# Shared convolution products seeded in a second PSUM bank, with the gate chain moved ahead

## The chip, the cores and the metric

The kernel runs on one core of a Trainium2 chip. The metric is the device time of one execution in microseconds. Engines: PE is TensorE (PEld its weight loads), DVE is VectorE, ACT is ScalarE, POOL is GpSimd, SP is the engine that issues most of the DMAs. Line numbers are those of the kernel before.

## The reference

An adaptive-LayerNorm block on x of shape (4, 1024, 2048), in float32. Six modulation vectors come from `c` (4 x 2048) and `wmod` (2048 x 6*2048):

```python
mod = (_silu(L0_c) @ L0_wmod).reshape(L0_c.shape[0], 6, 1, -1)
sa, ca, ga, sb, cb, gb = (mod[:, 0], ..., mod[:, 5])
ga = (2 * (ga >= 0) - 1) * jnp.maximum(jnp.abs(ga), 0.25)   # gb likewise
h = _layernorm(x, axis=-1) * (1 + ca) + sa
x = x + ga * _L0_attn_ref(h, ...)
h = _layernorm(x, axis=-1) * (1 + cb) + sb
x = x + gb * _L0_ffn_ref(h, ...)
```

`_L0_attn_ref` is a state-space layer: from 64 complex parameters it makes a kernel K of 2048 taps (four response sums over the states at 2048 frequencies, then an inverse FFT), convolves every row of h causally with K along the last axis, and adds `D * h`. `_L0_ffn_ref` is a linear layer of 2048 x 2048 with bias, with 16 low-rank updates of rank 16 added, each weighted by `coeffs * scales`.

## The kernel before

The 4096 rows of x are taken as 32 tiles of 128 rows, called rows here (r = 0 to 31). The kernel has two stages: in the first, every row goes through normalization, convolution, gate and residual, and is written to a scratch tensor `x1d`; in the second, 16 units of two rows go through the linear layer (`ffn_unit`, L750), written as seven products of half-size blocks.

**The convolution as matrix products.** The taps are laid out as a Toeplitz matrix of 128 x 128 blocks; even and odd blocks of the output are made from three families of products instead of four. `toeplitz` (L233) builds them: `s4` computes the response sums (`s4rp`, L175) and the taps, these go to DRAM (`kd`), come back as a shifted matrix `kb` (L258), are reversed by PE (`kbps`, L263), and become three pairs of f16 tensors, high and low part, `kh` and `kl` (L284, L285), one pair for each family f = 0, 1, 2.

**A row.** `stats` (L540) and `normalize` (`n`, L557) run on DVE. `conv_prep` (L566 on) transposes n on PE in four chunks of four blocks (`tp`, L578), ACT evacuates each with scale and shift (`t`, L582), DVE adds neighbouring blocks (`sm`, L590), and ACT and DVE split t and sm into f16 high and low parts `hc` and `hs` (L592, L593). `conv_mm` then runs 108 products in six groups (two halves q of the output, three families): family 0 from hs gives a sum that odd and even blocks share. It lies in PSUM tile `ya`, ACT copies it to SBUF (`qs`, L627), PE adds family 1 to it in place, and makes family 2 in `yb` alone; DVE adds `qs` to `yb` (L631). The odd blocks are then multiplied by the gate (L633), the even ones straight from `ya` (L640), and x is added with a running sum (L641). `conv_post` writes y to `x1d` and takes the second variance (L660).

**PSUM.** Three pools share the eight banks for the whole kernel: `acc` with five banks (all products), `tps` with two (transposes and small products), `mps` with one (`modps`).

**Before the gate is known.** `wmod` is 48 MB for its first three sections, read by 48 loads into two pools of three buffers each (`wm`, `wms`) and multiplied in L317 (`modps`). Section 1 (scale) comes first, then the shift, then the gate. Rows 0 and 1 (`EARLY = 2`) are convolved meanwhile without shift and gate, their products alternating with modps products (`pace`, `ROWC`). `shift_conv` makes the convolution of the shift (`gsp`, L397) and `shift_add` (L414) adds it to both rows. When section 2 is summed, `mod_gate` computes the gate on DVE and ACT (L342 to L347), `gate_tile` spreads it over the partitions by products with rows of the identity (`gps`, L674, `gat`, L675), and `conv_late` (L650, L651) finishes rows 0 and 1. Row 2's convolution runs at the same place; the constant `GCOL` says how many of its columns may stand ahead of gps in PE's order.

**The order of the work.** A scheduler orders each engine's instructions from the program text; `tc.issue_after(ins)` keeps what is traced inside it behind `ins` on that engine, as an order and not as a wait. Inside `conv_mm`, `tick` is called ten times a row, and each call does what `PLAN` says for it: N a part of the next row's `conv_prep`, P the `conv_post` of the row before, T statistics, F the first part of the row after next, S one step of the fill. The fill is the work for the second stage: the low-rank weights are prepared (`prep_lora`), merged into the linear weights in eight parts (`merge`, `lps`, L486, `we`, L488, `wch`, L514), and the other three sections of wmod are multiplied.

Of the kernel before, what the change touches and what calls it, by code (L numbers as in the profile page):

```python
# [24 lines left out]
P = 128  # L25
D = 2048
# [8 lines left out]
class Net:  # L35
    def __init__(self, ctx, tc, io):
        self.ctx, self.tc, self.nc, self.io = ctx, tc, tc.nc, io
        self.cst = ctx.enter_context(tc.tile_pool(name="cst", bufs=1))
        self.dram = ctx.enter_context(tc.tile_pool(name="scr", bufs=1, space=DRAM))
        self.acc = ctx.enter_context(tc.tile_pool(name="acc", bufs=ACC, space=PSUM))  # L40
        self.tps = ctx.enter_context(tc.tile_pool(name="tps", bufs=TPS, space=PSUM))
        self.mps = ctx.enter_context(tc.tile_pool(name="mps", bufs=1, space=PSUM))
# [33 lines left out]
    def s4(self, pool):  # L76
# [69 lines left out]
        rp = self.tps.tile([P, 16, 8], F32, tag="t", name="s4rp")  # L146
        w = 512
        yield
        cps = [[self.acc.tile([P, w], F32, tag="a", name="s4cs") for _ in range(2)] for _ in range(2)]
# [16 lines left out]
        for n, (cc, sc) in enumerate(cps):  # L166
# [4 lines left out]
            yield  # L171
            for c in range(w // P):
                out = rp.rearrange("p (h g) v -> p g h v", h=2)[:, 4 * n + c]
                for i, x in enumerate((wr[n], wi[n])):
                    nc.tensor.matmul(  # L175
                        out, x[:, ds(P * c, P)], cf[:, i],
                        start=(n, c, i) == (0, 0, 0), stop=(n, c, i) == (1, 3, 1), skip_group_check=True,
                    )
        r = T([P, 8, 16], "s4R")
        v.tensor_copy(r.rearrange("p v k -> p k v"), rp)  # L180
# [52 lines left out]
    def toeplitz(self, pool):  # L233
# [23 lines left out]
        src = bass.AP(tensor=kd.tensor, offset=kd.offset + 1, ap=[[1, P], [1, D]])  # L257
        nc.gpsimd.dma_start(out=kb, in_=src)  # L258
        self.kb = kb
        yield  # L260
        for q in range(4):
            ps = self.acc.tile([P, 512], F32, tag="a", name="kbps")
            nc.tensor.matmul(ps, rev, kb[:, ds(512 * q, 512)], start=True, stop=True)  # L263
            (v.tensor_copy if q % 2 else nc.scalar.copy)(kb[:, ds(512 * q, 512)], ps)
# [4 lines left out]
        self.kf = {}  # L269
        for f in (0, 2, 1):  # L270
            hi = self.kpool.tile([P, HC * P], F16, tag=f"kh{f}", name=f"kh{f}")
            lo = self.kpool.tile([P, HC * P], F16, tag=f"kl{f}", name=f"kl{f}")
            h3, l3 = (x.rearrange("p (m t) -> p m t", t=P) for x in (hi, lo))
            if f == 0:
                src = ev
            else:
                src = pool.tile([P, 2, 512], F32, tag="kdif", name="kdif")
                src = src.rearrange("p a (c t) -> p (a c) t", t=P)
                if f == 1:
                    v.tensor_scalar(src[:, 0:1], ev[:, 0:1], -1.0, None, MUL)  # L280
                    v.tensor_tensor(src[:, 1:], od[:, 0 : HC - 1], ev[:, 1:], SUB)
                else:
                    v.tensor_tensor(src, od, ev, SUB)
            v.tensor_copy(h3, src)  # L284
            v.tensor_tensor(l3, src, h3, SUB)  # L285
            self.kf[f] = hi, lo
        yield
# [36 lines left out]
    def mod_column(self, pool, home, name, plus_one):  # L324
# [3 lines left out]
        nc.scalar.copy(row, self.modps)  # L328
# [9 lines left out]
    def mod_gate(self, pool, name, bias=None):  # L338
# [8 lines left out]
        v.scalar_tensor_tensor(g, g, 1.0, m, SUB, MUL)  # L347
# [62 lines left out]
    def shift_add(self, pool, ys):  # L410
        g = pool.tile([P, D], F32, tag="gat", name="gsb")
# [55 lines left out]
    def merge(self, pool, tmp, c):  # L467
# [11 lines left out]
        for h in range(2):  # L479
            for q in range(4):  # L480
                ps = self.acc.tile([P, 512], F32, tag="a", name="lps")
# [54 lines left out]
    def stats(self, pl, x, tag):  # L536
# [8 lines left out]
        if tag in ACTNORM:  # L545
            mb = pl["sm"].tile([P, 1], F32, tag="mb" + tag, name="mb" + tag)
            v.scalar_tensor_tensor(mb, mv[:, 0:1], -1.0, rs, MUL, MUL)
            return mb, rs
        return mv, rs

    def normalize(self, pl, x, st, tag):
        n = pl["n"].tile([P, D], F32, tag="n", name="n" + tag)
        m, rs = st
        if tag in ACTNORM:
            self.nc.scalar.activation(n, x, AF.Identity, bias=m, scale=rs)
        else:
            self.nc.vector.tensor_scalar(n, x, m[:, 0:1], rs, SUB, MUL)  # L557
        return n
# [6 lines left out]
    def conv_prep(self, pl, r, x, st, out, shift=True):  # L565
# [8 lines left out]
        for c0 in range(0, NC, 4):  # L574
# [16 lines left out]
            for (hi, lo), src, sl in ((hc, t, slice(c0, c0 + 4)), (hs, sm, slice(c0 // 2, c0 // 2 + 2))):  # L591
                nc.scalar.copy(hi[:, sl], src)  # L592
# [3 lines left out]
    def conv_mm(self, pl, hs, x, tick, early, pace):  # L596
        nc, v = self.nc, self.nc.vector
        hc, hs = hs
        y = pl["y"].tile([P, D], F32, tag="y", name="y")
# [5 lines left out]
        def family(ps, f, q, first):  # L605
            pf = ps.rearrange("p j t -> p (j t)")
            last = 4 * q + 3
            for i in range(last + 1):
                o = P * max(0, i - 4 * q)
                k0 = P * max(0, 4 * q - i)  # L610
                with pace(3 * (512 - o)):
                    for x, z in ((0, 0), (0, 1), (1, 0)):
# [3 lines left out]
                            start=first, stop=(i == last and (x, z) == (1, 0)), skip_group_check=True,  # L616
                        )
                        first = False
# [3 lines left out]
        for q in range(2):  # L622
            jj = slice(4 * q, 4 * q + 4)
            pa = self.acc.tile([P, 4, P], F32, tag="a", name="ya")
            family(pa, 0, q, True)
            qs = pl["t"].tile([P, 4, P], F32, tag="qs", name="qs")
            self.lasta = nc.scalar.copy(qs, pa)  # L627
            tick()
            pb = self.acc.tile([P, 4, P], F32, tag="a", name="yb")
            family(pb, 2, q, True)  # L630
            self.lastv = v.tensor_tensor(yv[:, jj, 1, :], pb, qs, ADD)  # L631
            if not early:
# [534 lines left out]
```

## Time and profile before

| | |
|---|---|
| median of 3 runs | 2139.6 us (2136.27 to 2143.98) |
| profiled execution, its own time | 2141.87 us |
| its span | 2140.1 us |
| PE busy | 2082.4 us (97%) |
| DVE busy | 1308.4 us (61%) |
| ACT busy | 923.7 us (43%) |
| mean granted clock of PE | 0.988 |
| DMA | 484.11 MB, 226 GB/s |

The profile is one execution. The first stage takes the span's first 919 us (the first product of the second stage starts there), the second stage the rest. Digits in the profile's slices are tenths of a slice of 53.5 us. A group's row gives its busy time, the mean of one instruction in ns, and the engine's idle time before it with what ended it; in a timeline the last bracket is that idle time.

### The profile page before, as it was taken

The page shows a single profiled execution, that of the slowest core. Times are in us where ns is not written, and L with a number is a line of the kernel's source. Part 1 is how long each engine was busy: PE and PEld are TensorE (multiplying, and loading weights), DVE is VectorE, ACT ScalarE, POOL GpSimd, SP SyncE. Part 2 cuts the span into 40 slices and gives each one's busy share as a digit, 9 for nine tenths or more (in the row PEclk, how much of TensorE's full clock was granted, in tenths as well). Part 3 has the DMA queues.
Part 4 walks back from the last instruction along what each step waited for, and adds up shares of the span by engine and source line. Part 5 has one row for each costly group of instructions (what it writes and reads, how often), then busy time and mean ns, then how long its engine had stood idle before and what let it go on. Part 6 is the DMA issues. An engine that isn't in the chain of part 4 may idle for free.

```text
span 2140.1 us, 28438 instructions
## 1 busy us (share of the span) xinstructions
PE 2082.4 (97%) x11113; PEld 1026.1 (48%) x11113; DVE 1308.4 (61%) x2353; ACT 923.7 (43%) x1695; POOL 6.3 (0%) x18
## 2 busy tenths in 40 slices
PE   7898999999999999999999999999999999999998
PEld 2344455555555555554545545555444444444444
DVE  5439898898979999665565565575533323332323
ACT  1325876677767777745454555555200000000000
POOL 0000000000000000000000000000000000000000
PEclk7999999999999999999999999999999999999999
DMA  9977566787776554387564564564794645454542
GB/s 401 373 307 278 225 227 265 285 310 262 276 278 227 187 192 173 139 346 258 190 241 180 202 240 179 203 235 172 283 341 163 192 151 167 164 170 165 177 157 69
DMA packets 127236, 484.11 MB, mean 226 GB/s; under 512 B 13608, under 2 KB 13768, under 8 KB 95998
## 3 DMA queue, kind: packets, MB, share of 16 engines
q1 hardware_dynamic: 126192, 477.55, 61.4%
q10 hardware_dynamic: 526, 2.63, 0.4%
q8 instruction: 87, 1.43, 0.3%
q0 software_dynamic: 384, 2.11, 0.2%
q14 instruction: 47, 0.39, 0.0%
HBM read 326.94 MB, written 155.30 MB: 225 GB/s over the span
## 4 chain that ended last, share of the span: by engine, by line
PE 67%; DVE 18%; ACT 6%; DMA 5%; issue 2%; SPq 0%; ACTq 0%; POOL 0%; DVEq 0%; POOLq 0%
PE fZ L750 22%; PE fY L750 15%; PE fX L750 15%; PE ya L614 5%; PE yb L614 3%; PE tp L700 3%; DVE wch L514 2%; PE modps L317 2%; DVE st L540 2%; DVE hc L593 2%; DVE y L641 2%; ACT x L660 2%; DMA wcd<-wch 1%; ACT t L582 1%; PE lps L486 1%
## 5 line engine op out<-in xcount | busy, mean ns | idle before, releaser
L750 PEld LDWEIGHTS <-lf 128*128 128x128 f16 x5376 | 526.0, 98 | 620.9 <-issue 1.4
L750 PE MATMUL fZ<-w,lf 128*128 128x512 f16 x2304 | 513.6, 379 | 0.8 <-ACT p L758 0.8
L750 PE MATMUL fX<-w,lf 128*128 128x512 f16 x1536 | 342.8, 379 | 0.0
L750 PE MATMUL fY<-w,lf 128*128 128x512 f16 x1536 | 342.0, 379 | 0.0
L614 PEld LDWEIGHTS <-hc 128*128 128x128 f16 x2304 | 215.3, 98 | 204.6 <-issue 41.6
L768 DVE TENSOR_TENSOR xo<-xo,gb 128x512 f32<-128x512 f32 x128 | 87.8, 690 | 238.7 <-DMA xo<-x1d 227.2
L582 ACT ACTIVATE t<-tp,sa,ca 128x128 f32<-128x128 f32 x480 | 188.1, 471 | 21.6 <-PE tp L578 12.9
L614 PE MATMUL ya<-kh,hs 128*128 128x512 f16 (+3 forms) x768 | 193.7, 326 | 3.7 <-DVE kh L284 2.6
L614 PE MATMUL ya<-kh,hc 128*128 128x512 f16 (+3 forms) x768 | 192.7, 328 | 3.8 <-ACT qs L627 3.6
L614 PE MATMUL yb<-kh,hc 128*128 128x512 f16 (+3 forms) x768 | 192.2, 327 | 1.8 <-DVE y L640 1.4
L758 ACT COPY p<-fZ 128x512 f32<-128x512 f32 x64 | 37.2, 581 | 286.8 <-PE fZ L750 272.1
L614 PEld LDWEIGHTS <-hs 128*128 128x128 f16 x1152 | 105.9, 98 | 108.6 <-issue 28.4
L758 ACT COPY p<-fX 128x512 f32<-128x512 f32 x32 | 18.7, 585 | 316.3 <-PE fX L750 210.4
L702 ACT ACTIVATE gt<-tp,sb,cb 128x256 f32<-128x256 f32 x256 | 124.9, 576 | 60.8 <-PE tp L700 60.8
L317 PE MATMUL modps<-wm,sct 128*32 128x512 f32 x768 | 118.8, 662 | 14.1 <-DMA wm<-in_wmod 14.1
L614 PE MATMUL ya<-kl,hc 128*128 128x512 f16 (+3 forms) x384 | 125.8, 328 | 0.0
L614 PE MATMUL ya<-kl,hs 128*128 128x512 f16 (+3 forms) x384 | 125.1, 326 | 0.7 <-DVE kl L285 0.7
L614 PE MATMUL yb<-kl,hc 128*128 128x512 f16 (+3 forms) x384 | 125.6, 327 | 0.0
L773 DVE TENSOR_TENSOR fin<-fX,gb 128x512 f32<-128x512 f32 x32 | 22.1, 692 | 128.4 <-PE fX L750 128.3
L593 DVE TENSOR_TENSOR hc<-t,hc 128x512 f16<-128x512 f32 x128 | 87.5, 684 | 6.6 <-ACT hc L592 6.4
L486 PE MATMUL lps<-lbh,lac 128*128 128x512 f16 x256 | 86.3, 379 | 1.2 <-DVE we L488 1.2
L578 PE MATMUL tp<-ident,n 128*128 128x128 f32 x512 | 79.3, 280 | 8.1 <-ACT t L582 6.3
(264 smaller groups left out, 2228.0 us busy)
## 6 DMA issues: line engine op xcount, KB each, us to landing
wm<-in_wmod SPq DMA_DIRECT2D x96, 1024.0 KB
lfd<-lf SPq DMA_DIRECT2D x112, 512.0 KB
lf<-lfd SPq DMA_DIRECT2D x112, 512.0 KB
x<-in_x SPq DMA_DIRECT2D x32, 1024.0 KB
x1d<-y SPq DMA_DIRECT2D x32, 1024.0 KB
x<-x1d SPq DMA_DIRECT2D x32, 1024.0 KB
xo<-x1d SPq DMA_DIRECT2D x128, 256.0 KB
out<-xo SPq DMA_DIRECT2D x128, 256.0 KB
```

The costliest lines, as they stand in the source:

```text
L317: self.last = self.nc.tensor.matmul(self.modps[32 * g : 32 * g + 32, :], self.sct[:, j].rearrange("p r b -> p (r b)"), w[:, ds(512 * g, 512)],
L486: nc.tensor.matmul(ps, la[:, x, k, h], y[:, k, osl], start=(n == 0), stop=(n == 5))
L514: v.tensor_tensor(hl[:, :, 1, :], tv, hl[:, :, 0, :], SUB)
L578: nc.tensor.transpose(tp[:, k], n[:, ds(P * (c0 + k), P)], self.ident)
L582: nc.scalar.activation(t[:, k], tp[:, k], AF.Identity, bias=self.sa[:, c, b : b + 1], scale=self.ca[:, c, b : b + 1],)
L593: v.tensor_tensor(lo[:, sl], src, hi[:, sl], SUB)
L614: nc.tensor.matmul(pf[:, o:512], h, self.kf[f][z][:, ds(k0, 512 - o)], start=first, stop=(i == last and (x, z) == (1, 0)), skip_group_chec ...
L700: nc.tensor.transpose(tp[:, c, r], xs[r][:, ds(P * (c0 + c), P)], self.ident)
L702: nc.scalar.activation(t[:, c0 + c], tp[:, c], AF.Identity, bias=self.sb[:, c0 + c, b : b + 1], scale=self.cb[:, c0 + c, b : b + 1],)
L750: nc.tensor.matmul(ps[name], lf[i][:, k, x, :], wc[i][k // 4][:, k % 4, y, :], start=(first and n == 0), stop=(n == 3 * HC - 1), skip_grou ...
L758: nc.scalar.copy(t, ps[name])
L768: v.tensor_tensor(x, x, self.gbias[:, h], ADD)
```

## The change

- **PSUM**: in the first stage the pools are `cps` (tags pa and pb, two banks each), `tps` (three banks) and `mps`; `acc` and a two-bank `tps` are opened for the second stage only. kbps and lps move from `acc` to `tps`, s4's first products (`s4cs`) to `cps`.
- **Convolution**: ACT copies the shared sum from bank pa to bank pb, and PE adds family 2 to pb there, without a start flag. The DVE addition of qs is gone. From row 2 on, both halves' shared products come first, then the rest; for rows 0 and 1 half after half.
- **Response sums**: the coefficients are the weights and the responses the moving operand (four products of 16 x 512), followed by an ACT copy and eight small transposes.
- **Toeplitz parts**: kb is loaded, reversed and split in two halves of 1024 columns; the f16 casts (`kh`) go to ACT. The halves stand inside row 0's `conv_prep`.
- **Gate**: `gate_tile` stands before the shift adds, which are queued behind the gate's last DVE operation; `GCOL` is 30000. x of rows 0 and 1 is read a second time into wms buffers (`xl`), rows 4 and 5 are loaded early, row 2's y (`y2`) lies in kb's place, and the fill's pools are opened in row 3.
- **Order**: row 1's statistics and `conv_prep` are stepped by row 0's ticks; `PLAN` has eight S instead of nine.

```diff
-        for q in range(2):
+        def shared(q):
+            pa[q] = self.cps.tile([P, 4, P], F32, tag="pa", name="ya")
+            family(pa[q], 0, q)
+            pb[q] = self.cps.tile([P, 4, P], F32, tag="pb", name="yb")
+            self.lasta = nc.scalar.copy(pb[q], pa[q])
+            tick()
+
+        def rest(q):
             jj = slice(4 * q, 4 * q + 4)
-            pa = self.acc.tile([P, 4, P], F32, tag="a", name="ya")
-            family(pa, 0, q, True)
-            qs = pl["t"].tile([P, 4, P], F32, tag="qs", name="qs")
-            self.lasta = nc.scalar.copy(qs, pa)
-            tick()
-            pb = self.acc.tile([P, 4, P], F32, tag="a", name="yb")
-            family(pb, 2, q, True)
-            self.lastv = v.tensor_tensor(yv[:, jj, 1, :], pb, qs, ADD)
...
+            for e, f, ps in ((1, 2, pb[q]), (0, 1, pa[q])):
+                family(ps, f, q)
+                if early:
+                    nc.scalar.copy(yv[:, jj, e, :], ps)
+                else:
+                    self.lastv = v.tensor_tensor(yv[:, jj, e, :], ps, gv[:, jj, e, :], MUL)
...
+        for f, q in ((shared, 0), (rest, 0), (shared, 1), (rest, 1)) if early else (
+            (shared, 0), (shared, 1), (rest, 0), (rest, 1)
+        ):
+            f(q)
...
+            sp = self.tps.tile([16, w], F32, tag="t", name="s4sp")
+            for i, x in enumerate((wr[n], wi[n])):
+                nc.tensor.matmul(sp, cf[:, i].rearrange("p h v -> p (h v)"), x, start=(i == 0), stop=(i == 1))
+            sr = wq[n][0:16]
+            nc.scalar.copy(sr, sp)
             for c in range(w // P):
...
+                nc.tensor.transpose(rp[:, 4 * n + c], sr[:, ds(P * c, P)], self.ident[0:16, 0:16])
...
+        for half in range(2):
+            m = ds(4 * half, 4)
+            for q in range(2):
+                ps = self.tps.tile([P, 512], F32, tag="t", name="kbps")
+                sl = ds(1024 * half + 512 * q, 512)
+                nc.tensor.matmul(ps, rev, kb[:, sl], start=True, stop=True)
+                (v.tensor_copy if q else nc.scalar.copy)(kb[:, sl], ps)
+            for f in (0, 2, 1):
+                hi, lo = (x[:, m] for x in kf[f])
...
+                nc.scalar.copy(hi, src)
+                v.tensor_tensor(lo, src, hi, SUB)
...
-PLAN = ("PNSL", "NL", "NSL", "NTL", "SL", "SL", "SL", "SL", "FSL", "SSL")
+PLAN = ("PNL", "NSL", "NSL", "NTL", "SL", "SL", "SL", "SL", "FSL", "SL")
...
-GCOL = 11000
+GCOL = 30000
...
+    xl = []
+    with tc.issue_after(k.lastw.ins):
+        for r in range(EARLY):
+            load(r + 4)
+        for r in range(EARLY):
+            xl.append(wms.tile([P, D], F32, tag="wm", name="xl"))
+            nc.sync.dma_start(out=xl[r], in_=io["x"][ds(P * r, P), :])
+    k.gat = k.gate_tile(pl["g"], 0)
     take(nxt, 40)
-    k.shift_add(pl["g"], [ys[r][0] for r in range(2)])
...
+    with tc.issue_after(k.gated.ins):
+        k.shift_add(wms, [ys[r][0] for r in range(2)])
+    y2 = stp.tile([P, D], F32, tag="kb", name="y2")
```

## The prediction

> **What bounds the kernel now.** I read the page's engine shares and slices first, then a table of stretches that I cut at the landmarks of the code, then the timeline of DVE and PE where the table shows a hole, then PE's waits in the long stretch behind it.
>
> ```profile
> PE 2082.4 (97%) x11113; PEld 1026.1 (48%) x11113; DVE 1308.4 (61%) x2353; ACT 923.7 (43%) x1695; POOL 6.3 (0%) x18
> PE   7898999999999999999999999999999999999998
> DVE  5439898898979999665565565575533323332323
> ```
>
> TensorE is busy for 97%; all its idle time is 2140.1 - 2082.4 = 58 us. The change removes no product, so it can win only idle time of PE and time in which PE runs at half clock. DVE's digits are 8 and 9 from slice 5 to slice 16: where it is late, PE is late with it. The stretches (us, then busy us of PE, PEld, DVE, ACT, POOL, the granted clock, the DMA share):
>
> ```profile
> 52.00:77.00 25.00, 18.85 (x90) 7.77 (x89) 18.97 (x42) 9.38 (x28) 0.35 (x1) 0.89 0.95 384
> 77.00:159.00 82.00, 79.79 (x507) 33.38 (x507) 23.55 (x53) 21.96 (x58) 1.51 (x3) 0.94 0.83 329
> 159.00:175.00 16.00, 6.08 (x13) 2.18 (x9) 11.38 (x18) 0.85 (x3) 0.00 (x0) 0.68 0.92 351
> 175.00:203.00 28.00, 27.05 (x172) 15.10 (x171) 28.00 (x62) 19.94 (x40) 0.00 (x0) 1.00 0.56 189
> 203.00:245.00 42.00, 39.23 (x239) 19.52 (x237) 35.30 (x91) 36.48 (x74) 0.51 (x1) 0.96 0.76 290
> 245.00:919.00 674.00, 661.17 (x4078) 355.91 (x4077) 600.29 (x1251) 480.25 (x982) 0.41 (x1) 1.00 0.64 235
> ```
>
> 77 to 159 (rows 0 to 2 and the shift and gate rows of wmod) has PE full and DVE mostly idle. Then comes the hole: PE works 6 of 16 us while the gate is made. Then DVE is full for 28 us without a break. From 245 to 919 PE idles 13 us in 674. What makes the hole, on DVE and then on PE:
>
> ```profile
> 159.05 2.29 DVE L414 TENSOR_TENSOR y<-y,gsb 128x2048 f32<-128x2048 f32 x1 [7.87 <-ACT y L638]
> 161.26 2.46 DVE L540 BATCH_NORM_STATS2 st<-x 128x6 f32<-128x512 f32 x4
> 165.13 1.35 DVE L557 TENSOR_SCALAR n<-x,mv,rs 128x2048 f32<-128x2048 f32 x1
> 166.39 0.68 DVE L342 COPY mg<-modps 128x512 f32<-128x512 f32 x1
> 168.57 0.69 DVE L347 SCALAR_TENSOR_TENSOR mg<-mg,mg 128x512 f32<-128x512 f32 x1
> ...
> 169.31 5.81 PE L674 MATMUL gps<-mg,ident 128*128 128x512 f32 x8 [9.93 <-DVE mg L347]
> ```
>
> The last modps product ends at 159.4. The gate's copy (L342) could run then, but it stands behind a shift add that waited for row 1's last copy, and behind row 3's statistics: 7.0 us late. PE, behind gps in order, idles 9.93 us.
>
> **Part 1, gate chain first.** In the changed order DVE has row 3's statistics and n, ready long before, ahead of the gate, both shift adds behind it. PE has 102,912 columns of f16 products ahead of the last modps instead of 93,312, and 7,680 more between it and gps. A 512-column product takes 216 ns (24 in 5.18 us on the chain), so 9,600 columns are 4.05 us and 7,680 are 3.2 us. The last modps ends at 159.4 + 4.05 - e, with e what part 2 wins: 161.4 for e = 2. The gate chain takes 2.9 us (166.39 to 169.26), 3.6 with the one statistics instruction now inside it: gate at 165.0, about when PE's 3.2 us of products end. PE's idle goes.
>
> gps itself: 5.81 us at a granted clock of 0.68 over the stretch. The Trainium skill, "TensorE: Matmul & The Clock Gate", Part 1, says that the array falls to half rate after about 3.4 us of idleness and rises again after about as much work. By the row 5.8 us stay, by the rule about 3.4 (estimate), since PE now comes to gps busy. I take 3.4. The same rule also speaks against the change: if PE then waits for DVE, it falls again.
>
> It will wait, and this is where I differ from the plain gain of 12.3 us (9.9 + 2.4). From the gate on, DVE must do, in its new order and until row 4's n (L557) is done: gate chain rest and four gat 4.9 us (0.81 each, statistics between), four products times gat 2.7 (0.68), two shift adds 4.5 (2.29), four L650 and four L651 9.8 (1.28, 1.22), row 3's sm, hc, hs 5.5 (0.42, 0.68, 0.42, each four times, overlapped starts), two L641 2.4, n 1.35, small ones 1.5: 32.6 us. Row 4's n ends at 165.0 + 32.5 = 197.5; before, it ended at 202.5. At that point of PE's order as much PE work is done in either (141.9 against 141.6 us, counting products at their row's spacing). So 5.0 us are won, not 12.3: DVE was idle before 159 and full after, and the shift adds are moved to the full side. PE's stall, some 8 us around 180 to 191 for row 3's second chunk of hs, and a half clock there, lie under this wait and cost nothing more; without it they would cost up to 5 us. Bounds 0 to 8.
>
> **Part 2, start (e).** The response sums: before, 32 narrow products, 23.5 to 32.0 with a modps group between. After, eight passes of 512 columns f32; the nearest row, kbps, shows 5.4 us for eight at the slow clock, plus two ACT copies on the path (0.58 each) and eight 16-column transposes. I take 0.5 us later (bounds 1.3 earlier, 1.0 later). kb comes in two halves: 8 KB of kd took 5.1 us to land, 1 MB of kb 9.3, so half saves 2.1 us. kbps now stands ahead of row 0's transposes, which were early anyway. The six f16 casts go from DVE (0.69 per 1024) to ACT (about 0.62 per 512, 3.7 us). Row 0's first product needs ACT for kh and t: about 66.6 instead of 68.5. Row 0's second family now waits for the copy into PSUM, behind ACT's t and hc, about 70.4 instead of 73.1. Row 1's n: 16.6 us of DVE work from 57.7, 74.3 instead of 76.2. PE gets to row 1's transposes at about 75.2 with 0.95 us more products done, instead of 76.9: e = 2 (0 to 4); it enters above through the gate.
>
> **Part 3, shared products in PSUM.** Removed: one of DVE's two passes for odd blocks.
>
> ```profile
> L631 DVE TENSOR_TENSOR y<-yb,qs 128x512 f32<-128x512 f32 x64 | 43.8, 684 | 40.7 <-PE yb L614 38.6 <-ACT qs L627 2.1
> L633 DVE TENSOR_TENSOR y<-y,gat 128x512 f32<-128x512 f32 x60 | 40.9, 682 | 0.1
> ```
>
> 60 x 0.684 = 41 us of DVE go in rows 2 to 31; the multiply now reads yb. ACT's qs copy (592 ns) becomes a copy from PSUM to PSUM. No row shows one; I take 0.6 (0.4 to 1.2), and its cover is 24 products (4.3 us) or 12 and 12 (3.3 us). The four early adds become ACT copies of 0.61. In the long stretch DVE has slack, so 41 us of DVE are worth only PE's waits:
>
> ```profile
> PE tp L578 <- ACT t L582: 5.4, 6, 1.7
> PE ya L614 <- ACT qs L627: 2.6, 4, 1.2
> PE yb L614 <- DVE y L640: 1.4, 1, 1.4
> PE lps L486 <- DVE we L488: 1.2, 1, 1.2
> ```
>
> The second and third (4.0 us) go, since copies now have over 3 us and pb its own banks. Of the first, half (2.7), for three transpose banks instead of two; but lps moves into the same three. Costs: with two banks for each of pa and pb, a row's second shared product needs the bank of the row before, as soon as DVE has multiplied it. PE's new order puts 1.0 to 5.5 us between; the timeline of before shows 0.7 to 4.6 us from a row's last product to the end of L640, once 7.1. Against each other that is up to 8 us of stalls, with a lighter DVE less: I take 2.5. Net 4 (-4 to 7). Between 203 and 245 PE loses 2.8 us plus 1.7 to half clock, where row 5's hs came late: of this 1.5 (0 to 4).
>
> The Trainium skill, "PSUM — Partial Sum Buffer", The four PSUM rules, says that writes by ScalarE leave the bank's written bits alone, so that a product without start adds to them only where an earlier product had set the bits; its remedy is a product with the identity. At kbps's 0.68 us a pass (5.4 us for eight, slow clock), or half of that, 64 such seeds of two passes would be 44 to 87 us. The change does without: s4cs now opens all four banks at the very start and nothing restarts pb. So I count 0; no row shows it, and an overwrite would take the same time.
>
> **Other edits.** Reloading x for rows 0 and 1 (2 MB, SP) and prefetching rows 4 and 5 come behind the last wmod load at 143.7, where DMA falls to 51 to 210 GB/s: 0, unless gsb, now in a wmod buffer, is late (it took 7.5 us; it has until 173), each us then being one of DVE's whole queue. y2 delays the fill's start to row 3, and eight steps a row instead of nine end it about three rows later, still before row 30: 0; the loads of la then come close to their use on ACT, in front of row 5's t, at most 3 us. The PSUM pools switch at 919, where the first fX waits for one multiply: 0 (up to 1). The second half, 919 to 2140, is unchanged.
>
> **Sum.** 5.0 + 1.5 + 4 = 10.5 us. The profiled execution took 2141.87 us (span 2140.1), 2.3 above the median of 2139.6; from the median: 2129. About 0.3% (6.4 us) is what a measurement of this kernel can tell from no change.
>
> **Rivals.** (a) DVE's backlog drains faster than I count and the hole's 12.3 us stay won, with e = 4 and all of the removable waits: gain 15 to 24, about 2120. For it: 41 us less DVE work; against it: DVE's 28.00 of 28. Chance 0.24. (b) The gate's gain is eaten whole and part 3 nets nothing: gain 0 to 6, about 2136. For it: PE at 98% from 245 on. 0.18. (c) Slower: the bank for the second shared product. If DVE answers the row's last product later than PE's cover, PE stands still in each of 29 rows; at 0.58 us a row it takes 17 us and turns the forecast to 2146. For it: eleven of 29 rows have 2.15 us of cover or less, and lps queues for the transpose banks too. Against: a median answer of 1.8 us with the heavier DVE. 0.12. The forecast, gain 6.4 to 15: 0.46. So faster 0.70, same 0.18, slower 0.12. The range 2117 to 2142 takes in (b), most of (a), and the near edge of (c).
>
> **What would show it.** Right: gps with under 1 us of idle before it at about 165, taking about 3.5 us; PE idle some us between 178 and 198 on hs of row 3 and n of row 4; row 4's n at about 197.5; no wait on qs; DVE busy near 1265. Wrong: PE waiting for L640's successor in many rows (c); ACT waiting for la or DVE for gsb near 175 to 215; row 1's transposes not before 77.

## The result, and the profile after

Changed kernel: 2148.8 us median (2143.59 to 2151.99, 9 runs), against 2140.2 for the kernel before on the same chip. The ratio is 1.0036, with a 95% interval from 1.0022 to 1.005. It is slower by some 8 us where 10.5 us less was forecast, and lies above the range of 2117 to 2142. The profiled execution took 2148.1 us (span 2146.3). From here on, line numbers are those of the changed kernel unless a fence shows another.

The page first, engine totals and slices:

```profile
PE 2076.7 (97%) x11097; PEld 1020.4 (48%) x11097; DVE 1277.3 (60%) x2291; ACT 931.3 (43%) x1707; POOL 6.7 (0%) x19
PE   6998899999999999999999999999999999999998
DVE  5528788887887899756565565565432323332323
```

PE is busy 5.7 us less than before, gps at full clock among it, and yet the span is 6.2 us longer: PE idles 69.6 us instead of 57.7. In PE's slices the second is fuller (9, 8 before), and the fifth, 215 to 268 us, is emptier (8, 9 before). The stretches (us, then busy us of PE, PEld, DVE, ACT, POOL, the granted clock, DMA):

```profile
52.00:77.00 25.00, 22.96 (x137) 9.70 (x135) 20.16 (x48) 17.15 (x49) 0.35 (x1) 0.95 1.01 420
77.00:159.00 82.00, 78.56 (x509) 33.04 (x502) 23.19 (x58) 20.50 (x52) 1.51 (x3) 0.96 0.98 395
159.00:175.00 16.00, 15.71 (x93) 7.76 (x91) 15.77 (x21) 6.28 (x17) 0.00 (x0) 1.00 0.21 75
175.00:203.00 28.00, 21.49 (x117) 10.03 (x118) 27.53 (x70) 19.67 (x44) 0.00 (x0) 0.82 0.79 281
203.00:245.00 42.00, 34.52 (x200) 17.42 (x199) 23.35 (x64) 25.60 (x48) 0.34 (x1) 0.92 0.77 297
245.00:919.00 674.00, 651.85 (x4011) 353.24 (x4009) 573.27 (x1187) 482.57 (x983) 0.41 (x1) 0.99 0.63 229
```

From 159 to 175 PE is busy 15.7 of 16 us, 6.1 before. From 175 to 203 it idles 6.5 us; a stall was forecast here, but its longest gap is a wait for a load of wmod, and only the next two are waits for row 3's hs:

```profile
177.86 1.94 PE L325 MATMUL modps<-wm,sct 128*32 128x512 f32 x8 [3.07 <-DMA wm<-in_wmod]
181.24 0.39 PE L616 MATMUL ya<-kh,hs 128*128 128x256 f16 x1 [1.44 <-ACT hs L593]
...
183.36 0.50 PE L616 MATMUL ya<-kh,hs 128*128 128x256 f16 x2 [1.51 <-DVE hs L594]
```

Then comes what was not forecast: from 203 to 245 it idles 7.5 us (2.8 before) while DVE too is busy only 23 of 42 us (35 before), and from 245 on it idles 22 us (13 before). The end of the gate chain on DVE, then on PE:

```profile
158.62 0.67 DVE L355 SCALAR_TENSOR_TENSOR mg<-mg,mg 128x512 f32<-128x512 f32 x1
...
167.52 4.48 DVE L422 TENSOR_TENSOR y<-y,gsb 128x2048 f32<-128x2048 f32 x2
...
189.37 1.34 DVE L558 TENSOR_SCALAR n<-x,mv,rs 128x2048 f32<-128x2048 f32 x1
```

```profile
159.41 3.65 PE L685 MATMUL gps<-mg,ident 128*128 128x512 f32 x8
```

The last line has no idle time in front of it (9.93 us before), and takes 3.65 us instead of 5.81. Row 4's n ends at 190.7, 11.8 us earlier than before. The first loss after this lead starts on ScalarE, one row later:

```profile
202.18 0.40 ACT L593 CAST hs<-sm 128x256 f16<-128x256 f32 x1
211.43 1.91 ACT L440 ACTIVATE la<-la 128x2048 f32<-128x2048 f32 x1 [8.86 <-DMA la<-in_A]
...
215.23 0.58 ACT L632 COPY yb<-ya 128x512 f32<-128x512 f32 x1
...
225.76 0.20 ACT L69 ACTIVATE r_t<-r_v 128x1 f32<-128x1 f32 x1 [7.48 <-DVE r_v L68]
225.87 1.49 ACT L583 ACTIVATE t<-tp,sa,ca 128x128 f32<-128x128 f32 x4
```

ScalarE comes to the squares of A at 202.6 and stands before them for 8.86 us, since the 2 MB of the low-rank weights A (`la`) have not landed. Queued behind them are the second bank's seed (L632) and row 5's t (L583). Later it waits again, 7.48 us for a value from VectorE, and VectorE's timeline shows why:

```profile
215.97 0.17 DVE L51 TENSOR_SCALAR lsa_i<-lam 128x2 f32<-128x2 f32 x1 [6.89 <-ACT lam L441]
...
224.16 0.35 DVE L481 TENSOR_SCALAR laf<-laf,lsa_s 128x256 f32<-128x256 f32 x1 [4.16 <-DMA laf<-in_A]
```

VectorE waits for what ScalarE makes of A's squares, and then for the first slice of A (laf), a load that SyncE issued right behind A. r_v is queued behind it. TensorE waits for the seed and then for t:

```profile
215.86 0.38 PE L616 MATMUL yb<-kh,hc 128*128 128x512 f16 x1 [2.36 <-ACT yb L632]
227.06 1.12 PE L579 MATMUL tp<-ident,n 128*128 128x128 f32 x4 [5.07 <-ACT t L583]
```

These two gaps are 7.4 us. From 225.2 on the granted clock is at half for 6.8 us; PE is busy in 4.9 of them, which costs some 2.5 more (an estimate, half of 4.9).

SyncE shows why the load is late. Before, it was issued at 157.4 and ScalarE came to it at 193.8, without a wait:

```profile
157.37 0.40 SPq L426 DMA_DIRECT2D la<-in_A  x1
```

```profile
193.76 1.91 ACT L432 ACTIVATE la<-la 128x2048 f32<-128x2048 f32 x1
```

Now it is issued at 196.2:

```profile
189.48 0.33 SPq L667 DMA_DIRECT2D x1d<-y  x1
192.99 0.33 SPq L563 DMA_DIRECT2D x<-in_x  x1
193.36 1.43 SPq L432 DMA_DIRECT2D lws<-in_coeffs  x2
194.83 1.24 SPq L432 DMA_DIRECT2D lws<-in_scales  x2
196.18 0.40 SPq L434 DMA_DIRECT2D la<-in_A  x1
```

Row 2's output y2 lies in the Toeplitz buffer, so the pools of the fill open only once y2 is done, and in SP's queue the load stands behind y2's own store, a load of x that waits 3.2 us for ScalarE, and four small loads of `coeffs` and `scales`. PE's waits from 245 to 919 (us in total, times, longest):

```profile
PE yb L616 <- ACT yb L632: 5.1, 3, 2.6
PE lps L494 <- DVE we L496: 4.0, 4, 2.7
PE lps L494 <- ACT t L583: 3.7, 3, 1.6
PE tp L579 <- DVE we L496: 2.4, 2, 1.5
PE tp L579 <- DVE n L558: 2.3, 2, 1.9
PE tp L579 <- ACT t L583: 1.6, 3, 1.0
PE ya L616 <- DVE y L642: 1.6, 3, 1.0
```

The waits on qs (2.6) are gone; waits on the seed (5.1) and waits of lps and the transposes on each other's readers have come: lps and the transposes take the banks of one pool in turn (a ring), and each waits until what lay in its bank has been read. The groups of L642 and L632 show what the seeding removed and what it costs:

```profile
L642 DVE TENSOR_TENSOR y<-yb,gat 128x512 f32<-128x512 f32 x60 | 40.9, 682 | 7.2 <-PE yb L616 7.1
L632 ACT COPY yb<-ya 128x512 f32<-128x512 f32 x64 | 37.6, 588 | 35.4 <-PE ya L616 33.5 <-DMA gbd<-mg 1.9
```

To compare kernels whose orders differ I use PE's lag: the time at which PE starts the first transpose of a row, less the PE work that stands ahead of it in that kernel's own order (216 ns for a 512-column f16 product, shorter ones in proportion, 265 for a modps product, 133 for a transpose, and so on from the traces). A row's step to the next column is what PE lost there to idleness or half clock; fX is the first product of the second stage. In us, each from one profiled execution:

```
kernel          row 1  row 4  row 5  row 6  row 8  row 24   fX
before           41.0   61.0   61.5   66.7   67.5   77.2   82.9
changed          33.4   48.9   48.8   59.4   60.1   76.4   87.0
a1_la_later      33.8   53.0   52.7   52.4   59.7   71.8   80.8
a4_nine_s        34.1   50.2   50.0   69.1   69.8   84.0   93.6
b1_no_seed       35.2   50.4   51.2   52.0   55.5   66.5   75.0
b6_la_nine_s     33.0   48.4   48.4   49.2   57.2   70.8   84.7
c1_front_only    32.0   48.5   49.0   49.6   59.0   71.3   77.0
a3_before_lps_t  35.8   53.5   53.5   55.6   56.2   71.0   76.4
```

Nearly equal orders differ by up to 4 us here (rows 1 to 5 of the changed kernel and of a1), so a single difference under that is not read. The changed kernel is 12 us ahead at row 4. It adds 10.6 of lag in row 5 (before: 5.2), about the 9.9 us of gaps and half clock above. From row 8 to fX it adds 27, where the kernel before adds 15: this second loss is the larger one in this pair of traces. At fX it is 7.0 us late (925.9 against 918.9).

### The profile page after: what moved, and what is told of

It reads as the page before. It is cut to its first block, busy times and chain, and to the rows that moved or that the text cites. A ratio compares the mean times of both kernels' runs of the same rounds, so it can differ in the third digit from the quotient of the medians.

```text
span 2146.3 us, 28330 instructions
## 1 busy us (share of the span) xinstructions
PE 2076.7 (97%) x11097; PEld 1020.4 (48%) x11097; DVE 1277.3 (60%) x2291; ACT 931.3 (43%) x1707; POOL 6.7 (0%) x19
## 4 chain that ended last, share of the span: by engine, by line
PE 64%; issue 27%; DMA 4%; DVE 3%; ACT 2%; SPq 0%; POOLq 0%; POOL 0%; DVEq 0%; ACTq 0%
PE fZ L761 23%; PE fX L761 15%; PE fY L761 15%; PE ya L616 3%; PE tp L711 3%; PE yb L616 2%; DMA wm<-in_wmod 2%; PE modps L325 2%; DMA x<-x1d 1%; DMA laf<-in_A 1%; PE tp L579 0%; DVE y L645 0%; ACT t L583 0%; DVE st L548 0%; ACT x L701 0%
## 5 line engine op out<-in xcount | busy, mean ns | idle before, releaser
L583 ACT ACTIVATE t<-tp,sa,ca 128x128 f32<-128x128 f32 x480 | 187.5, 469 | 19.8 <-PE tp L579 19.7
L548 DVE BATCH_NORM_STATS2 st<-x 128x6 f32<-128x512 f32 x128 | 83.8, 681 | 20.0 <-DMA x<-in_x 19.9
```

Of the source, the lines that this page charges most:

```text
L548: v.bn_stats(st[:, q], x[:, ds(512 * q, 512)])
L583: nc.scalar.activation(t[:, k], tp[:, k], AF.Identity, bias=self.sa[:, c, b : b + 1], scale=self.ca[:, c, b : b + 1],)
```

## The experiments

Each kernel was timed beside the kernel before on the same chip, and its ratio is against that, so ratios can be set beside one another, medians less well. A difference of two ratios is sure to 0.14 to 0.18%, 3 to 4 us.

**Later fill (a1_la_later).** In row 3 the fill makes only its first step, which loads A; its other steps begin in row 4.

```diff
-            if r > EARLY and calls[0] % 2 == 0:
+            if r > EARLY and calls[0] % 2 == 0 and (calls[0] == 10 or r > EARLY + 1):
```

> The changed kernel, but the fill makes only its first step (the load of A) in row 3 and goes on in row 4, so that ScalarE reaches the squares of A about one row (22 us) later. Theory: in the changed kernel ScalarE waits 8.86 us for this load in front of row 5's transposes, which costs TensorE two gaps (2.36 and 5.07 us) and a half clock of about 7 us. Without it the start of fX lies 5 to 8 us earlier than 925.9 and the time is about 2143 to 2144. Rival: the row that was delayed had slack behind it (the lead at row 4 would have been lost to VectorE's backlog anyway); then the gaps at 216 and 227 come back elsewhere before 260 and the time moves by less than 2 us.

2136.95 us (13 runs), ratio 0.9977 (0.9965 to 0.9989). This alone turns the sign: 0.59% below the changed kernel's ratio, about 12.6 us (8.7 to 16.5), more than expected. The load is issued at 198.2, no earlier than in the changed kernel. ScalarE comes to it 18 us later and has no wait:

```profile
219.66 1.54 ACT L583 ACTIVATE t<-tp,sa,ca 128x128 f32<-128x128 f32 x4
221.04 1.96 ACT L440 ACTIVATE la<-la 128x2048 f32<-128x2048 f32 x1
```

In row 5 the lag grows by nothing instead of 10.6 us. But 6.9 of it come in row 6: at row 8 this trace stands where the changed kernel's stands (59.7 and 60.1), and the 6.2 us by which it leads at fX come after that. It is the slowest of the 13 runs (2142.45 us). So the edit is worth 12.6 us; how much of that is the wait, and how much that every early step of the fill comes a row later, this pair does not separate.

**lps in a bank of its own (a2_lps_bank).**

```diff
-    k.tps = k.psum(ps1, "tps", 3)
+    k.tps = k.psum(ps1, "tps", 2)
+    k.lps = k.psum(ps1, "lps", 1)
...
-                ps = self.tps.tile([P, 512], F32, tag="t", name="lps")
+                ps = self.lps.tile([P, 512], F32, tag="l", name="lps")
```

> The changed kernel, but the sums of A and BfT (lps) get a PSUM bank of their own and the transposes keep two banks instead of three. Theory: about 10 us are lost between 245 and 919 because lps and the transposes stand in one ring of three banks, each waiting for what the other's reader does. With the ring parted the waits on lps fall from 7.8 us to under 2, transposes wait for ScalarE's t again about as in the kernel before (5.4 us), and the stretch gains 3 to 6 us: 2143 to 2146. Rival: it is the copy in front of the second family (5.1 us of waits) and the later fill that take the time; then the stretch gains under 2 us or loses some, 2147 to 2150.

2149.5 us (6 runs), ratio 1.0033 (1.0021 to 1.0045): as the changed kernel. The theory falls, the time is in the rival's span. ScalarE waits for A here too (7.5 us), and PE's waits only change names:

```profile
PE tp L579 <- ACT t L583: 7.9, 9, 2.1
PE lps L494 <- DVE we L496: 4.3, 7, 1.2
PE ya L616 <- DVE y L642: 4.1, 5, 1.7
```

**lps among the transposes, in the kernel before (a3_before_lps_t).**

```diff
-        self.acc = ctx.enter_context(tc.tile_pool(name="acc", bufs=ACC, space=PSUM))
-        self.tps = ctx.enter_context(tc.tile_pool(name="tps", bufs=TPS, space=PSUM))
...
+    k.acc = k.psum(ps1, "acc", 4)
+    k.tps = k.psum(ps1, "tps", 3)
...
-                ps = self.acc.tile([P, 512], F32, tag="a", name="lps")
+                ps = self.tps.tile([P, 512], F32, tag="t", name="lps")
```

> The kernel before, but with lps in the transposes' ring, which has three banks as in the changed kernel, and the products' ring four instead of five (five and two again in the second half). Everything else, the order and the shared products' copy and add, stays. Theory: sharing the ring costs by itself, 5 to 10 us between 245 and 919: 2145 to 2150. Rival: it costs only together with the seeding or the shifted fill: 2138 to 2142, with fewer waits of transposes for t since there are three banks.

2138.4 us (22 runs), ratio 0.9981 (0.9973 to 0.9989): faster than before, in the rival's span. Sharing the ring is no cost by itself. This trace gains its time in rows 1 to 4 (53.5 at row 4, before 61.0) and from row 8 to fX loses 20 us, 5 more than before; the waits there show the price of four product banks:

```profile
PE ya L613 <- ACT qs L626: 9.9, 8, 2.1
PE tp L577 <- DVE we L487: 2.8, 3, 1.5
```

**Nine fill steps (a4_nine_s).** `"SL")` at the end of PLAN becomes `"SSL")`.

> The changed kernel with nine fill steps a row as before, not eight. Theory: the fill now ends about three rows earlier, so that ScalarE's casts of it no longer stand in front of the copies of the shared products in rows 28 to 31, where the second stage's work begins (gaps of 2.65 and 1.88 us and a half clock at 832): gain 3 to 5 us, 2144 to 2146. Rival: denser fill steps bring as many waits in rows 6 to 25 as they take away behind: within 2 us of the changed kernel, 2147 to 2151.

2154.2 us (5 runs), ratio 1.0058 (1.0045 to 1.007): both expectations missed, it is 5 us slower than the changed kernel. The wait for A is there as well, and as long as in the changed kernel, but the lag grows by 19 us in row 5:

```profile
212.32 1.91 ACT L440 ACTIVATE la<-la 128x2048 f32<-128x2048 f32 x1 [8.90 <-DMA la<-in_A]
```

**No seeding from row 2 on (b1_no_seed),** on top of the later fill.

```diff
-                            start=(f == 0 and (i, x, z) == (0, 0, 0)), stop=(i == last and (x, z) == (1, 0)),
+                            start=(f in fresh and (i, x, z) == (0, 0, 0)), stop=(i == last and (x, z) == (1, 0)),
...
+        fresh = (0,) if early else (0, 2)
...
-            self.lasta = nc.scalar.copy(pb[q], pa[q])
+            if early:
+                self.lasta = nc.scalar.copy(pb[q], pa[q])
+            else:
+                qs[q] = pl["t"].tile([P, 4, P], F32, tag="qs", name="qs")
+                self.lasta = nc.scalar.copy(qs[q], pa[q])
...
+                    if e:
+                        v.tensor_tensor(yv[:, jj, e, :], ps, qs[q], ADD)
+                        ps = yv[:, jj, e, :]
```

> The changed kernel with the later fill of a1_la_later, and from row 2 on without the second bank's seeding: ScalarE copies the shared products to SBUF, the second family starts its bank afresh, VectorE adds the two and then multiplies, as in the kernel before; banks and the order of families stay. Theory after the first four runs: between row 6 and fX the changed kernel and its later-fill version lose 6 to 11 us more than the kernel before, because the second family now waits for a copy (3.6 to 5.1 us) that only VectorE's add waited for; without the seeding this comes back and the time falls by 4 to 6 us, to about 2132. Rival, as forecast: the seeding's 41 us less on VectorE are worth 4 us; without it the time rises to about 2141. Third: both cancel, within 2 us of 2137.

2136.8 us (5 runs), ratio 0.9970 (0.9958 to 0.9982), beside 0.9977 with the seeding: the third expectation. About 41 us of DVE work, put back, cost nothing that these runs can tell.

**The old order of chunks with the seeding (b2_pair_order),** on top of the later fill: rows take `(shared, 0), (rest, 0), (shared, 1), (rest, 1)`.

> The changed kernel with the later fill, but every row takes its chunks one after the other (shared product, its two families, then the second shared product and its families), as rows 0 and 1 do and as the kernel before did. Seeding and banks stay. Theory: the two shared products at the start of a row make the second one wait for VectorE's answer to the row before (2.9 us of waits) and crowd two copies and hc, hs on ScalarE; in the old order that goes, but the first chunk's second family then has only the shared product's copy in front of it with no product to cover it, 0.6 to 1.2 us in each of 30 rows: 20 to 35 us slower, 2157 to 2172. Rival: the transposes and other small products of the plan cover it, and the time is within 3 us of 2137.

2152.4 us (6 runs), between the two expectations; ratio 1.0046 (1.0034 to 1.0058). The order moves ScalarE's squares forward again, so that it waits 4.71 us for A in this kernel too, and the total can't be put down to the order alone. From row 8 to fX, past that wait, the lag grows by 30 us, 21 in a1, and the waits name the seed:

```profile
PE yb L616 <- ACT yb L632: 11.7, 13, 3.2
```

With the seeding, the old order costs more of these waits (11.7 us; 3.6 in a1), as the theory had it; the 20 to 35 us expected for 30 rows were too much.

**Four and three banks, lps with the products, in the kernel before (b3_before_t3).**

> The kernel before with four banks for the products and three for the transposes (five and two again in the second half), lps staying with the products. In a3_before_lps_t this split, with lps among the transposes, brought 3.7 us, with row 1's transposes at 71.0 instead of 76.9. Theory: it is the third transpose bank that works in rows 0 and 1; then row 1's transposes start at 71 to 72 here too, though the products' ring of four with lps in it loses some us after 245: 2138 to 2143. Rival: the earlier start was the kb transfer landing earlier by chance; then row 1 starts at 75 to 77 and the time is 2142 to 2150.

2147.4 us (12 runs), ratio 1.0023 (1.0013 to 1.0032); row 1's transposes start at 76.8. The theory falls: the third transpose bank does nothing for rows 0 and 1. That chance was the reason, as the rival says, is not shown: DVE's kk (the taps before they go to DRAM) is 3.1 us earlier in a3 than in the kernel before, with the same order of instructions, and why stays open. a3 is 0.42% faster than this kernel; that holds the move of lps out of the product banks and the earlier row 1 together.

**Later fill and nine steps (b6_la_nine_s).**

> The changed kernel with the later fill and nine fill steps a row instead of eight. Nine steps alone made the changed kernel 5 us slower. Theory: that was only because ScalarE then came still earlier to the late load of A (the loss in row 5 was 19 us instead of 10); with the later fill nine steps cost nothing, and the end of the fill before row 28 brings 1 to 3 us: 2134 to 2137. Rival: nine steps crowd VectorE and ScalarE everywhere; then it is 3 to 5 us slower than the later fill alone: 2140 to 2142.

2145.7 us (21 runs), ratio 1.0018 (1.0012 to 1.0025), slower than both expectations. Against a4 (1.0058) the later fill is worth 0.40% here, 8.6 us, and this pair shows it where the wait was: the traces differ by 12.6 us of lag at row 8 (69.8 and 57.2) and by 8.9 at fX. Against a1 (0.9977) the ninth step costs 0.41%, 8.8 us, and this is where the slower rival of the forecast, the bank of the second shared product, shows:

```profile
PE ya L616 <- DVE y L642: 10.5, 7, 3.6
```

**The change without its first item (c1_front_only),** on top of the later fill: the kernel before's `conv_mm` in all rows, five banks for products and lps, two for transposes, PLAN of before less its last S.

> The change without its first item: gate chain first, Toeplitz parts in halves, response sums with coefficients as weights, eight fill steps, and the later fill of a1_la_later; but shared products, their order and add, and the PSUM rings (five banks for products and lps, two for transposes) as in the kernel before, in all rows. Theory: the front part alone is worth its lead of 8 to 9 us at row 5, and the long stretch then costs no more than in the kernel before (15 us from row 8 to fX, against 19.5 to 21.5 with the rings parted two, two and three): 2128 to 2133. Rival: the third bank for the transposes made the lead; then row 1 starts at 75 to 77 and the time is 2137 to 2141.

2134.5 us (7 runs), between the two expectations; ratio 0.9965 (0.9953 to 0.9978), the lowest of all. Row 1's transposes start at 70.7, so the lead does not need the third bank. The shared products in PSUM, with their rings and order, bring nothing that these runs can tell (a1: 0.9977; the difference, 2.6 us in favour of leaving them out, is within its uncertainty). From row 8 to fX this kernel loses 18 us, not 15.

**Eight steps in the kernel before (c2_before_8s).**

> The kernel before with eight fill steps a row instead of nine (the last tick makes one instead of two), nothing else. With the later fill, nine steps were 8.6 us slower than eight. Theory: fewer steps a row thin out ScalarE's and VectorE's work in rows 5 to 25, which is full in the kernel before too: 2134 to 2138. Rival: it matters only with the parted rings, or the fill then runs into rows 28 to 31 and costs there: 2141 to 2146.

2139.8 us (14 runs), ratio 0.9991 (0.9981 to 1.0001): between the two expectations, at most 4 us. The step count matters less here than with the parted rings.

**Three banks for the shared product (c3_pa3),** transposes and lps two, on top of the later fill.

> The changed kernel with the later fill, and three banks instead of two for the shared products; the transposes and lps share two instead of three. Theory, the slower rival of the forecast: a row's second shared product waits for VectorE's answer to the row before; with a third bank this wait (2.9 us in a1_la_later) goes to nothing, and the transposes' waits rise by about as much: 2135 to 2140. Rival: the transposes and lps need their third bank more: 2142 to 2150.

2139.8 us (14 runs), ratio 0.9994 (0.9985 to 1.0004), within the theory's span and slower than a1, by a difference (0.17%) just outside its uncertainty. No wait of a shared product for L642 is left in the stretch, and the transposes' waits for t rise from 2.9 to 6.1, as the theory had it:

```profile
PE tp L579 <- ACT t L583: 6.1, 8, 1.6
PE yb L616 <- ACT yb L632: 2.4, 2, 1.9
```

**c1 with the rings of a3 (c4_front_43).**

> As c1_front_only, but with four banks for the products and three for the transposes with lps among them, as in a3_before_lps_t, which alone brought 3.7 us. Theory: both gains add: 2126 to 2131. Rival: the two gains are one and the same lead at row 4; then 2134 to 2139.

2135.5 us (12 runs), ratio 0.9974 (0.9963 to 0.9985), in the rival's span: the gains don't add.

**A late load in the kernel before (d1_before_la_late).** Its first fill step in row 2 is left out, and one element of row 2's output is copied into A's buffer ahead of the load.

```diff
-    with tc.issue_after(k.lastw.ins):
-        next(fill)
...
+        v.tensor_copy(a[:, 0, 0:1], self.late[:, 0:1])
         nc.sync.dma_start(out=a, in_=io["A"].rearrange("c p k h d -> p c k (h d)"))
```

> The kernel before with the load of A bound to row 2's finished output by a copy of one element into its buffer, and its first fill step no longer ahead of row 2, as the changed kernel's pools force it; the squares on ScalarE stand some 25 instructions further back in its queue than before, in front of row 5's last chunk. Theory: the late load costs in this kernel too, as ScalarE comes to it before it has landed: 3 to 12 us more, 2144 to 2153. Rival: the squares' place moves with the load, so that ScalarE finds it landed, as in the later-fill version: 2138 to 2143.

2146.9 us (22 runs), ratio 1.0016 (1.0007 to 1.0025), 3.4 us, at the edge of the theory's span but not by its mechanism. The load is issued at 200.4 and ScalarE uses it at 212.6 without a wait, as the rival had it; what PE waits for is a wmod load and then t:

```profile
235.96 1.57 PE L317 MATMUL modps<-wm,sct 128*32 128x512 f32 x2 [4.04 <-DMA wm<-in_wmod]
239.74 1.12 PE L579 MATMUL tp<-ident,n 128*128 128x128 f32 x4 [2.22 <-ACT t L583]
```

So the late load with its moved fill step costs 1.5 to 5.4 us (by the interval) even where ScalarE doesn't wait for it. The wait itself was not reproduced in the kernel before.

**The wait over all traces.** Four kernels wait for A: the changed one, a2, a4, and b2, which has the later fill and yet waits. Their fX starts at 925.9 to 932.5 (b2's order costs time of its own). The other eight versions of the changed kernel (three of them without its first item), all with the later fill, have no such wait, and their fX starts at 913.9 to 923.6.

**A thinner fill in rows 5 and 6 (d2_front_r7, d3_la_r7):** `R0 = 7` instead of 5 in c1 and in a1.

> c1_front_only with the fill at half density up to row 6 instead of row 4. In all later-fill versions a lead of 9 to 12 us over the kernel before stands at row 6, and 4 to 9 us of it go in the next row: ScalarE has the squares and scalings of BfT there, SyncE issues seven loads of wmod in a burst, and TensorE waits 4.1 us for one of them and 3.7 us for transposed data. Theory: the fill's start is crowded into rows 5 and 6 since it began later; spread out it costs 3 to 6 us less, 2128 to 2132. Rival: the burst comes whenever the fill's products start, and the longer fill runs into rows 28 to 31: 2134 to 2139.

> a1_la_later with the fill at half density up to row 6 instead of row 4. Same theories as for the version with the front part alone. Theory: 3 to 6 us less than a1_la_later, 2131 to 2134. Rival: no gain, or a loss since this version's fill already ends latest of all: 2136 to 2142.

2143.4 us (22 runs), ratio 1.0007 (0.9998 to 1.0017), slower than c1's 0.9965; and 2139.3 (14 runs), 0.9982 (0.9974 to 0.9991), as a1. d3 is in its rival's span, d2 slower than both of its spans. Thinning the fill in rows 5 and 6 brings nothing back; what takes the rest of the lead stays open.

## Why the prediction was wrong, by its own steps

**Part 1, the gate chain: right in kind, too small.** From the finished gate to row 4's n I counted 32.5 us of DVE work; it took 31.4 (159.3 to 190.7). The stall and the half clock came where they were put (gaps of 3.07, 1.44, 1.51 and 0.67 us between 175 and 187; the granted clock from 175 to 203 is 0.82), but only the 2.95 us in the middle were for row 3's hs; the first gap was a wmod load that the forecast did not have, the last a bank. gps took 3.65 us, near the 3.4 that I took by the rule of the Trainium skill ("TensorE: Matmul & The Clock Gate", Part 1) and not the 5.8 of the row. In c1 less idleness than that rule's 3.4 us was enough:

```profile
161.17 5.40 PE L676 MATMUL gps<-mg,ident 128*128 128x512 f32 x8 [2.06 <-DVE mg L355]
```

There PE is busy 1.44 us from 159.0 to 162.5, and from 162.5 to 166.0 the granted clock is 0.51; the measurement decides. The term that was mis-sized is e: the last modps ended at 155.3 where 159.4 + 4.05 - 2 was forecast, so e was 8.1 (6.1 in a1, whose order is the same up to there). Of it, 4.7 us stand at row 1's transposes (72.2 instead of 76.9); the others come by row 3 and are not assigned. The gain at row 4 was 11.8 us, not 5.0. One reading of the slices was loose and changes nothing: slice 12 of DVE's digits before is a 7.

**Other edits, "the loads of la ... at most 3 us": the step that failed.** I saw that the load came close to its use in front of row 5's work, priced it as at most 3 us of ScalarE, and counted it as 0. ScalarE's wait was 8.86 us. Its queue held the seed and t, both on PE's path, and VectorE's queue was held twice, for 6.89 us by a value made from A and for 4.16 us by the second load of A. The sign named in "What would show it", ACT waiting for la near 175 to 215, came true. Row 5 took 10.6 us of lag, 5.4 more than before. In the runs the later fill, which takes the wait away, is worth 12.6 us with eight steps and 8.6 with nine, each sure to 3 to 4 us; the share of the wait alone is not separated. All four kernels that wait for A lie above the kernel before (1.0033 to 1.0058). So do b3, b6 and d1 without such a wait, but lower (1.0016 to 1.0023). The order that removed the hole made it worse: ScalarE's squares stood behind work that now came sooner, the load behind an output of row 2. With this term at 12.6 in place of 0 the sum would have come to a loss of 2 us, not a gain of 10.5; the measured loss is some 6 us larger, the balance of part 3 below and the larger gain of part 1.

**Other edits, "eight steps a row instead of nine: 0".** With the later fill they gain 8.8 us, without it 4.7 (just outside its uncertainty), in the kernel before at most 4 (c2). The forecast left out a term in its own favour.

**Part 3, net +4: the second step that failed.** The waits on qs went, as said, and the waits on the seed (5.1 us) took their place. The copy from PSUM to PSUM took 588 ns, as assumed. But from row 8 to fX, where 4 us were to be won, the changed kernel loses 11.5 us more than the kernel before; with the later fill it is 5.7 more (a1), with qs and the add put back 4.1 (b1), without the whole item 2.6 (c1), each from one trace. In the times of the runs neither the seeding (b1) nor the whole item (c1) brings anything. DVE is busy 31 us less than before (1277 against the 1265 forecast), and no gain of PE's came of it. PE's waits in this stretch name PSUM banks and their readers, and the partings of the eight banks tried here (a2, a3, b3, c3) moved these waits from one pool to another. "Of this 1.5" was to be won in row 5, where 5.4 more than before were lost, for the reason above.

**What stays open.** With the later fill the kernel is 4.9 us (a1) or, less the first item, 7.5 us (c1) faster than before, out of a lead of some 9 to 12 us at row 5. The rest goes in row 6 and in the long stretch, in small waits on wmod loads, t and banks that differ from kernel to kernel; a thinner fill in rows 5 and 6 (d2, d3) did not bring it back, and no cause was found. Why the changed kernel loses more than a1 from row 8 on is open too.

**Rivals.** (c) was the right sign by a wrong cause: its wait is 1.6 us in the changed kernel, and reaches 10.5 only with nine steps (b6). That part 3 nets nothing, half of (b), fits the runs. The measured time lay outside the range because no case held both a wait at the new place of a load and a loss in the long stretch.

## What to carry to other kernels

When a change lets a buffer live longer, list the loads that wait for that buffer's pool, find where each is first used, and read what stands behind that use in the engine's queue: a late load costs what is queued there, not its own wait (the same wait of 8.9 us went with 10.6 us of lag in one kernel and 19 in another). A lead won on one engine brings the next use of such a load nearer while the load itself stays where it was, so a gain and this cost come together. Moving the first use, with the steps behind it, one row later changed the time more than any other edit made to the changed kernel here.

## What was not expected of the hardware

The 2 MB load of A took 15.2 us from its issue to ScalarE's start on it (196.18 to 211.43), in stretches with a DMA share of 0.79 and 0.77; in d1 at most 12.2, at a share of 0.71. ScalarE's copy from PSUM to PSUM (128x512 f32) costs as much as one to SBUF, 588 against 592 ns. A wait of 2.06 us in front of gps was enough for half clock (c1). Eight steps of the interleaved fill a row instead of nine made the kernel with the later fill 8.8 us faster although the work is the same.
